# A lookup-and-MLP kernel: one token in 64 fetched row by row by SyncE, output stores on ScalarE, the last five tiles as blocks of one

## The chip, the cores and the metric

The kernel runs on one core of a Trainium2 chip. The metric is the device time of one execution in microseconds (us). Before the change it is 5179.57 us, the median of three runs (5178.03 to 5191.77). A core has five engines with a queue of instructions each, executed in order: TensorE (PE; its weight loads are shown as PEld), VectorE (DVE), ScalarE (ACT), GpSimd (POOL) and SyncE (SP), which computes nothing and issues DMAs. They meet through semaphores. Sixteen DMA engines move the data. A DMA issued by POOL has its descriptors written by software on POOL; one issued by SP or ACT goes through a hardware queue.

## The reference, cut to what matters

For each of 16384 samples, 32 token rows of 300 numbers are averaged, three groups of 20 small-table rows of 64 numbers are averaged, four more rows are looked up, and the 748 features go through three layers and a sigmoid. All of it is float32.

```
tok = word_emb[token_idx].mean(axis=1)          # 32 of 50000 rows of 300
e1 = emb_mh1[mh1_idx].mean(axis=1)              # 20 of 1000 rows of 64; e2, e3 likewise
emb = jnp.concatenate([tok, e1, e2, e3, o1, o2, o3, o4], axis=1)
wide = wide_mh1[mh1_idx].sum(axis=(1, 2)) + ...
h = jax.nn.relu(emb @ W1 + b1)                  # 748 -> 1024
h = jax.nn.relu(h @ W2 + b2)                    # -> 512
h = jax.nn.relu(h @ W3 + b3)                    # -> 256
return jax.nn.sigmoid(h @ Wd + bd + wide)
```

## The kernel before, in words

The samples are cut into 128 tiles of 128. Three streams of work are written out side by side, in one loop over `n_steps` = 128 x 11 + 27 = 1435 steps (L632); nothing reorders them afterwards, so what is written first on an engine runs first there.

**Small tables.** In the 11 steps of a tile the kernel counts how often each table row occurs in each sample. `one_hots` (L341) makes one-hot vectors on DVE for the next step (L348) and scales a part of them on ACT (L355); `counts` (L358) multiplies them on PE (L366), and ACT moves the counts from PSUM to SBUF (L369). In the tile after, `small_sums` (L381) multiplies counts with the tables on PE, 138 matmuls a tile in four groups, each into the one `pg` buffer (L401), and DVE takes each group from there (L391). The one-hots have `HOT_BUFS` = 3 buffers.

**Tokens.** `tokens` (L273) works in groups of two tokens, 16 a tile. For each token POOL issues one indirect DMA that gathers 128 rows of 1200 bytes, one per partition (L283). Three groups later (`TOK_LAG`) `add_up` (L260) adds both rows to a running sum on DVE (L264, L266, L271). `TOK_BUFS` = 6 groups have buffers. The loop hands these out at an even pace:

```
toks.to(n_all * (step + 1) / n_steps)          # n_all = 128 * 16 + 3 groups
```

**Layers.** When a tile's features are complete, PE transposes them and DVE scales them into the block's `x` (L442, L446). A block is three tiles (384 columns), but the last two tiles are blocks of one. `mlp` (L521) runs the layers of a block on PE (L505), ACT applies bias and relu (L516). Its matmuls are spread over the steps until `deadline` (L607), the step at which the next block is ready; the last block of three has until 6 steps before the end. `finish` (L542) adds the wide term on DVE (L544), takes the sigmoid on ACT (L545) and stores the outputs with a DMA on SP (L547).

**SP's queue** holds the loads of indices for each two tiles (`load_indices`, L294: one `it` for the tokens, L299; two `ix` for the tables, L304), tables and weights at the start, and the output stores. The semaphores of DMAs issued by SP and ACT are eight, taken in turn; a DMA waits for the one that had the semaphore before it.

Of the kernel before, what the change touches and what calls it, by code (L numbers as in the profile page):

```python
# [8 lines left out]
F32 = mybir.dt.float32  # L9
BF16 = mybir.dt.bfloat16  # L10
FP8 = mybir.dt.float8e3
I32 = mybir.dt.int32
# [6 lines left out]
P = 128  # L19
N_TOK, TOK_D = 32, 300  # L20
# [3 lines left out]
TOK_GROUP = 2  # L24
TOK_LAG = 3
TOK_BUFS = 6
HOT_BUFS = 3
WAKE = 27
EARLY = 3
LAST_LAYERS = 6  # L30
BLOCK = 256
LAYER_TILES = 3
LAST_TILES = 2
HALF = P // 2
UPPER = 256.0
COUNT = 64.0
# [4 lines left out]
STEPS = -(-HALF // ONEHOT)  # L41
# [22 lines left out]
def kernel(  # L64
# [21 lines left out]
    nc = tc.nc  # L86
    B = out.shape[0]
# [6 lines left out]
    for f in SMALL:  # L94
        n = -(-tables[f].shape[0] // P)
# [3 lines left out]
    tokp = ctx.enter_context(tc.tile_pool(name="tok", bufs=TOK_BUFS))  # L99
# [3 lines left out]
    scp = ctx.enter_context(tc.tile_pool(name="sc", bufs=2))  # L103
    ohp = ctx.enter_context(tc.tile_pool(name="onehot", bufs=HOT_BUFS))
    cp = ctx.enter_context(tc.tile_pool(name="counts", bufs=2))
    gp = ctx.enter_context(tc.tile_pool(name="g", bufs=3))
    wp = ctx.enter_context(tc.tile_pool(name="wide", bufs=2))
    xp = ctx.enter_context(tc.tile_pool(name="x", bufs=2))
# [19 lines left out]
    NK = len(chunk_rows)  # L128
# [126 lines left out]
    n_groups = N_TOK // TOK_GROUP  # L255
    n_all = B // P * n_groups + TOK_LAG
# [2 lines left out]

    def add_up(t, q, rows):  # L260

        a, b = rows[:, 0:TOK_D], rows[:, TOK_D : 2 * TOK_D]
        if q == 0:
            nc.vector.tensor_add(tok_sum, a, b)  # L264
        else:
            nc.vector.tensor_add(tok_sum, tok_sum, a)  # L266
            to = tok_sum
            if q == n_groups - 1:
                to = features(t)[:, TOK_AT:G_COLS]
                summed.add(t)  # L270
            nc.vector.tensor_add(to, tok_sum, b)  # L271

    def tokens():  # L273

        under_way = []
        for n in range(n_all):
            if n < n_all - TOK_LAG:
                t, q = divmod(n, n_groups)
                it = token_indices[t // NSUB][:, t % NSUB, :].bitcast(U32)
                rows = tokp.tile([P, TOK_GROUP * TOK_D], F32, name="tok_rows")  # L280
                for r in range(TOK_GROUP):
                    j = q * TOK_GROUP + r
                    nc.gpsimd.indirect_dma_start(  # L283
                        out=rows[:, r * TOK_D : (r + 1) * TOK_D],
                        out_offset=None,
                        in_=word,
                        in_offset=bass.IndirectOffsetOnAxis(ap=it[:, j : j + 1], axis=0),
                    )
                under_way.append((t, q, rows))
            if n >= TOK_LAG:  # L290
                add_up(*under_way.pop(0))
            yield 1

    def load_indices(blk):  # L294

# [110 lines left out]
    def wide_term(g):  # L406
# [7 lines left out]
        )  # L414
        nc.vector.tensor_add(g[:, WIDE_AT : WIDE_AT + 1], wide, g[:, 0:1])

    class Block:

        def __init__(self, first, n):
            self.first, self.n, self.missing = first, n * P, NK * n
            if first + n < B // P:
                self.x = xp.tile([P, NK, N], F32, name="x")
            else:
                self.x = cp.tile([P, NK, n * P], F32, name="x_last", tag="counts")

        def transpose(self, t, ks):

# [91 lines left out]
    def mlp(block, part=None):  # L521


        n = block.n
        flush_rows()
        h1 = hp.tile([P, M1, N], F32, name="h1", tag="odd")
        yield from layer(h1, w1_sb, b1_sb, [block.chunk(k) for k in range(NK)], M1, part)
        h2 = hp.tile([P, M2, N], F32, name="h2", tag="even")
        yield from layer(h2, w2_sb, b2_sb, [h1[:, k, 0:n] for k in range(M1)], M2)
        flush_outputs()  # L530
        h3 = hp.tile([P, M3 + 1, N], F32, name="h3", tag="odd")
        yield from layer(h3, w3_sb, b3_sb, [h2[:, k, 0:n] for k in range(M2)], M3)
        po = ps_h.tile([1, N], F32, name="po", tag="ph")
        for k in range(M3):
            if k == M3 - 1:
                flush_outputs()
            nc.tensor.matmul(  # L537
                po[:, 0:n], wd_sb[:, k : k + 1], h3[:, k, 0:n], start=(k == 0), stop=(k == M3 - 1)
            )
            yield 1  # L540

        def finish():  # L542
            y = h3[0:1, M3, 0:n]
            nc.vector.tensor_add(y, po[:, 0:n], block.wide())  # L544
            nc.scalar.activation(y, y, AF.Sigmoid, bias=bd_sb)  # L545
            b0 = block.first * P
            nc.sync.dma_start(out=out[b0 : b0 + n, :].rearrange("n o -> o n"), in_=y)  # L547

        rows_out.append(finish)

# [50 lines left out]
    block_of = {}  # L601

    def ready(t):

        return max(-(-(n_groups * (t + 1) + TOK_LAG) * n_steps // n_all) + 1, (t + 2) * STEPS + 2)

    def deadline(block):  # L607

        last = block.first + block.n // P
        ahead = tiles - 1 - last  # L610
        if ahead == 1 and block.n > P:
            return n_steps - LAST_LAYERS
        return ready(ends[last] - 1) if ahead > 0 else n_steps

    def block_for(t):
        if t not in block_of:
# [7 lines left out]
    toks = Paced(tokens())  # L624
# [6 lines left out]
    layers, cnt, sums, waiting, complete = None, None, None, [], []  # L631
    for step in range(n_steps):  # L632
        t, i = divmod(step, STEPS)
        s = t % NSUB
        blk = t // NSUB + 1
        more = blk * NSUB < tiles
# [34 lines left out]
        if complete and (layers is None or layers.done >= layers.total or complete[0].first + complete[0].n // P < tiles - 1):  # L671
# [6 lines left out]
            begin, left = step, max(deadline(block) - step, 1)  # L678
        toks.to(n_all * (step + 1) / n_steps)
        if t < tiles and more and s == 1 and i == 5:  # L680
            next_sc, evict = key_columns(next_keys)
            later.append((step, evict))
        ahead = 0
        if sums:
            ahead = n_h * (i + 1) / STEPS - sums_done[i + 1]
# [65 lines left out]
```

## Time and profile before

| | |
|---|---|
| median of three runs | 5179.57 us |
| the profiled execution | 5177.48 us |
| its span | 5175.7 us |
| PE busy | 4786.2 us, 92% |
| POOL busy | 3875.7 us, 75% |
| DVE busy | 3732.3 us, 72% |
| ACT busy | 2719.7 us, 53% |
| mean busy share of the 16 DMA engines in mid-run | 0.47 |
| share of the granted TensorE clock | 0.99 |

A line of the costliest groups gives the source line, the engine, the operation, what is written and read, the count, then busy time and mean ns, then the idle time of the engine just before these instructions and what ended most of it ("issue": nothing that the profile shows). A line of waits gives who waited for whom: us in total, times, the longest. A timeline line gives start, duration, engine, line, what is written and read, the count, and in brackets the idle time before it. SPq is SP's queue of DMA issues.

### The profile page before, as it was taken

The numbers are of one execution on the slowest core, as the hardware profiler recorded it, in microseconds if no ns is written. First come the engines' busy times: TensorE is split into PE (matmuls) and PEld (weight loads), VectorE is DVE, ScalarE is ACT, GpSimd is POOL, SyncE is SP. The second block draws the span as 40 slices with busy tenths as digits, with TensorE's granted clock in tenths as the row PEclk, the third lists the DMA queues.
The fourth block names the chain that finished last, engine by engine and source line by source line (L and its number), as shares of the span: only waits on it lengthen the run. The fifth ranks groups of instructions, "written<-read, shape, count | busy, mean of one in ns | idle before, by whom it ended". The sixth has DMA issues, their size and how long they took to land.

```text
span 5175.7 us, 92043 instructions
## 1 busy us (share of the span) xinstructions
PE 4786.2 (92%) x34812; PEld 3524.4 (68%) x34812; DVE 3732.3 (72%) x6656; ACT 2719.7 (53%) x3538; POOL 3875.7 (75%) x4103
## 2 busy tenths in 40 slices
PE   7799999999999999999999999999999999999999
PEld 4666666667667666767666766666667666667666
DVE  6777777777777777777777777777777777777773
ACT  6555555555555555555555555555555555555551
POOL 6777777777777777777777777777777777777775
PEclk9999999999999999999999999999999999999999
DMA  7444444444444444444444444444444444444443
GB/s 193 125 126 125 125 126 125 126 125 125 125 126 124 126 125 126 125 126 125 125 126 124 126 124 126 125 126 124 126 125 125 126 125 126 125 125 125 125 124 86
DMA packets 253982, 651.96 MB, mean 126 GB/s; under 512 B 120135, under 2 KB 120691, under 8 KB 253535
## 3 DMA queue, kind: packets, MB, share of 16 engines
q0 software_dynamic: 196608, 629.41, 45.4%
q1 hardware_dynamic: 56927, 16.66, 1.4%
q8 instruction: 272, 4.46, 0.4%
q14 instruction: 175, 1.43, 0.1%
HBM read 645.59 MB, written 0.07 MB: 125 GB/s over the span
## 4 chain that ended last, share of the span: by engine, by line
PE 49%; DMA 17%; DVE 15%; issue 11%; POOL 7%; ACT 0%; DVEq 0%; POOLq 0%; ACTq 0%
PE ph L505 27%; DMA tok_rows<-in_word_emb_dram,it 17%; PE pg L401 14%; POOL tok_rows L283 7%; DVE hot L348 5%; PE pc L366 5%; DVE own L271 4%; DVE own L266 3%; DVE g L391 2%; PE po L537 1%; PE pc L442 1%; DVE own L264 0%; DVE x L446 0%; ACT hot L355 0%; DVE ix L317 0%
## 5 line engine op out<-in xcount | busy, mean ns | idle before, releaser
L283 POOL DMA_INDIRECT tok_rows<-in_word_emb_dram,it x4096 | 3874.8, 946 | 1258.2 <-issue 788.3
L355 ACT ACTIVATE hot<-hot 64x768 bf16<-64x768 bf16 (+1 forms) x1408 | 1155.4, 821 | 1689.3 <-DVE hot L348 1676.8
L401 PE MATMUL pg<-terms,cnt 128*128 128x195 bf16 x17664 | 1734.8, 248 | 324.7 <-DVE g L391 324.7
L401 PEld LDWEIGHTS <-cnt 128*128 128x128 fp8e3 x17664 | 1519.2, 98 | 50.8 <-issue 32.4
L505 PE MATMUL ph<-x,w_sb 128*128 128x384 f32 (+2 forms) x4128 | 1476.8, 490 | 17.4 <-DVE x L446 17.1
L348 DVE TENSOR_TENSOR hot<-own,sc 128x1656 bf16<-128x1656 bf16 (+1 forms) x1408 | 1392.9, 989 | 83.3 <-PE pc L366 3.7
L369 ACT ACTIVATE cnt<-pc 128x828 uint16<-128x828 f32 (+1 forms) x1408 | 1185.8, 842 | 420.5 <-PE pc L366 398.8
L505 PE MATMUL ph<-h,w_sb 128*128 128x384 f32 (+1 forms) x3520 | 1238.7, 488 | 0.0
L271 DVE TENSOR_TENSOR own<-own,tok_rows 128x300 f32<-128x300 f32 x1792 | 856.9, 478 | 400.8 <-DMA tok_rows<-in_word_emb_dram,it 354.3
L505 PEld LDWEIGHTS ph<-x,w_sb 128*128 128x128 f32 (+1 forms) x4128 | 718.6, 191 | 556.0 <-issue 203.9
L266 DVE TENSOR_TENSOR own<-own,tok_rows 128x300 f32<-128x300 f32 x1920 | 917.7, 478 | 246.4 <-DMA tok_rows<-in_word_emb_dram,it 188.6
L366 PEld LDWEIGHTS <-hot 128*128 128x128 bf16 x8192 | 597.5, 97 | 511.9 <-issue 285.6
L505 PEld LDWEIGHTS ph<-h,w_sb 128*128 128x128 f32 x3520 | 619.5, 193 | 434.3 <-issue 150.8
L366 PE MATMUL pc<-hot 128*128 128x138 bf16 x8192 | 731.8, 225 | 28.6 <-ACT hot L355 23.4
L516 ACT ACTIVATE h<-ph,b_sb 128x384 f32<-128x384 f32 (+1 forms) x611 | 349.7, 572 | 280.0 <-PE ph L505 260.1
L391 DVE TENSOR_REDUCE g<-pg 128x130 f32<-128x390 f32 (+1 forms) x512 | 261.1, 510 | 324.1 <-PE pg L401 321.7
L446 DVE TENSOR_TENSOR x<-pc,scale 128x768 f32<-128x768 f32 x127 | 121.2, 954 | 107.3 <-PE pc L442 106.5
L264 DVE TENSOR_TENSOR own<-tok_rows 128x300 f32<-128x300 f32 x128 | 61.2, 478 | 87.7 <-DMA tok_rows<-in_word_emb_dram,it 86.3
L442 PE MATMUL pc<-ident,g 128*128 128x128 f32 x762 | 106.4, 277 | 0.4 <-ACT cnt L369 0.4
L335 DVE COPY sc<-pc 128x512 bf16<-128x512 bf16 x64 | 44.1, 689 | 80.5 <-PE pc L331 80.4
L442 PEld LDWEIGHTS pc<-ident,g 128*128 128x128 f32 x762 | 84.5, 143 | 16.3 <-issue 7.7
L271 DVE TENSOR_TENSOR g<-own,tok_rows 128x300 f32<-128x300 f32 x128 | 60.2, 470 | 34.8 <-DMA tok_rows<-in_word_emb_dram,it 32.1
(56 smaller groups left out, 404.9 us busy)
## 6 DMA issues: line engine op xcount, KB each, us to landing
tok_rows<-in_word_emb_dram,it POOLq DMA_INDIRECT x4096
ix<-in_idx_dram SPq DMA_DIRECT2D x128, 32.0 KB
w_sb<-in_W_dram SPq DMA_DIRECT2D x6, 512.0 KB
raw<-in_mh_dram SPq DMA_DIRECT2D x4, 682.5 KB
it<-in_idx_dram SPq DMA_DIRECT2D x64, 32.0 KB
w_sb<-in_W_dram SPq DMA_DIRECT2D x1, 2048.0 KB
out_dram<-h SPq DMA_DIRECT2D x42, 1.5 KB
raw<-in_mh_dram SPq DMA_DIRECT2D x2, 227.5 KB
```

The source lines that it names most:

```text
L266: nc.vector.tensor_add(tok_sum, tok_sum, a)
L271: nc.vector.tensor_add(to, tok_sum, b)
L283: nc.gpsimd.indirect_dma_start(out=rows[:, r * TOK_D : (r + 1) * TOK_D], out_offset=None, in_=word, in_offset=bass.IndirectOffsetOnAxis(ap ...
L348: nc.vector.tensor_tensor(hot[:, 0 : 2 * rows, :].rearrange("p i (n d) -> p i n d", d=2), iota.rearrange("p (n d) -> p n d", d=2).unsqueez ...
L355: nc.scalar.activation(upper, upper, AF.Copy, scale=UPPER)
L366: nc.tensor.matmul(pc[:, k // n, at : at + n_h], hot[:, 2 * k, 0:P], hot[:, 2 * k + 1, :], start=True, stop=True)
L369: nc.scalar.activation(cnt[:, :, b : b + rows].rearrange("l h (g k) -> l h g k", g=2), pc[:, :, 0 : n * n_h].rearrange("l g (k h) -> l h g ...
L391: nc.vector.tensor_reduce(field_columns(features(t), pair), pg[:, 0:n, :].rearrange("p f (c d) -> p f d c", c=3), AX.X, ALU.add,)
L401: nc.tensor.matmul(pg[:, j, :], by_slice[:, h, :], terms[:, h, :], start=(h == h0), stop=(h == h1 - 1))
L442: nc.tensor.transpose(pt[:, j // n, j % n, :], g[:, c : c + P], ident)
L505: nc.tensor.matmul(ph[:, 0:n], weights[: src.shape[0], k, m * P : (m + 1) * P], src, start=(k == 0), stop=(k == len(srcs) - 1),)
L516: nc.scalar.activation(dst[:, m, 0:n], ph[:, 0:n], AF.Relu, bias=bias[:, m : m + 1])
```

## The change

In tiles 4, 6, 8, ... 126, POOL gathers 31 tokens instead of 32. The rows of the last token are fetched by SP: `load_column` brings the 128 indices onto one partition, `fetch` reads them into SP's registers, 16 at a time, and issues one DMA per row, with an address computed from the register. This is written out over 20 steps, from 24 steps before the tile's sum is due; the column's load comes 4 steps earlier. `add_up` takes the two operands of a group from wherever they are.

Output stores are issued by ACT. The one-hots have two buffers in place of three. Tokens are handed out at two groups a step for the first 24 steps and at (2051 - 48) / (1435 - 24) = 1.4196 a step after that. The last five tiles are blocks of one; the last block of three gets 20 steps for its layers, each single block 8; the singles' `x` lie in pairs in a buffer of the counts. In tile 1 the columns of the next keys come four steps later.

```
-HOT_BUFS = 3
+HOT_BUFS = 2
+FETCH_FROM = 4
+FETCH_STEPS = 20
+FETCH_AHEAD = 24
+COLUMN_AHEAD = 4
+LOADS = 16
-LAST_LAYERS = 6
-LAST_TILES = 2
+LAST_TILES = 5
+FRONT_STEPS = 24
+FRONT_PACE = 2.0
+BLOCK_STEPS = 20
+TILE_STEPS = 8
...
+    fp = ctx.enter_context(tc.tile_pool(name="fetched", bufs=2))
...
-        a, b = rows[:, 0:TOK_D], rows[:, TOK_D : 2 * TOK_D]
+        a, b = rows
...
+                    if j == N_TOK - 1 and t in fetched:
+                        rows.append(fetched.pop(t))
+                        continue
+                    rows.append(tok_rows[:, r * TOK_D : (r + 1) * TOK_D])
...
+    def load_column(t):
+        columns[t] = fp.tile([1, P], I32, name="column")
+        nc.sync.dma_start(
+            out=columns[t], in_=idx[t * P : (t + 1) * P, N_TOK - 1 : N_TOK].rearrange("n o -> o n")
+        )
+
+    def fetch(t):
+        rows = fp.tile([P, TOK_D], F32, name="fetched")
+        column = columns.pop(t)
+        for p0 in range(0, P, LOADS):
+            _, values = nc.values_load_multi_w_load_instructions(
+                column[:, p0 : p0 + LOADS],
+                engines=[mybir.EngineType.SP],
...
+            for i, value in enumerate(values):
+                p = p0 + i
+                nc.sync.dma_start(out=rows[p : p + 1, :], in_=word[bass.ds(value, 1), :])
+                if p == P - 1:
+                    fetched[t] = rows
+                yield 1
...
-            if first + n < B // P:
+            if first + n + 2 < B // P:
                 self.x = xp.tile([P, NK, N], F32, name="x")
             else:
-                self.x = cp.tile([P, NK, n * P], F32, name="x_last", tag="counts")
+                if first + 2 == B // P or not last_x:
+                    last_x[:] = [cp.tile([P, 2, NK, P], F32, name="x_last", tag="counts")]
+                self.x = last_x[0][:, (first + 1) % 2]
...
-            nc.sync.dma_start(out=out[b0 : b0 + n, :].rearrange("n o -> o n"), in_=y)
+            nc.scalar.dma_start(out=out[b0 : b0 + n, :].rearrange("n o -> o n"), in_=y)
...
+    front = FRONT_STEPS * FRONT_PACE
+    pace = (n_all - front) / (n_steps - FRONT_STEPS)
+    fetches = [(int(summed_at(t)) - FETCH_AHEAD, t) for t in range(FETCH_FROM, tiles, 2)]
...
-        ahead = tiles - 1 - last
-        if ahead == 1 and block.n > P:
-            return n_steps - LAST_LAYERS
-        return ready(ends[last] - 1) if ahead > 0 else n_steps
+        if last < tiles - LAST_TILES:
+            return ready(ends[last] - 1)
+        return begin + (BLOCK_STEPS if block.n > P else TILE_STEPS)
...
-        toks.to(n_all * (step + 1) / n_steps)
+        for at, t_f in fetches:
+            if step == at - COLUMN_AHEAD:
+                load_column(t_f)
+            if step == at:
+                fetching.append((at, Paced(fetch(t_f))))
+        for at, rows in list(fetching):
+            rows.to(P * (step + 1 - at) / FETCH_STEPS)
...
+        toks.to(tokens_by(step + 1))
-        if t < tiles and more and s == 1 and i == 5:
+        if t < tiles and more and s == 1 and i == (5 if t > 1 else 9):
```

More of the change, by code (lines that the diff above doesn't have):

```diff
@@ L279, in tokens @@
                 it = token_indices[t // NSUB][:, t % NSUB, :].bitcast(U32)
-                rows = tokp.tile([P, TOK_GROUP * TOK_D], F32, name="tok_rows")
+                tok_rows = tokp.tile([P, TOK_GROUP * TOK_D], F32, name="tok_rows")
+                rows = []
                 for r in range(TOK_GROUP):
                     j = q * TOK_GROUP + r
+                    if j == N_TOK - 1 and t in fetched:
+                        rows.append(fetched.pop(t))
+                        continue
+                    rows.append(tok_rows[:, r * TOK_D : (r + 1) * TOK_D])
                     nc.gpsimd.indirect_dma_start(
-                        out=rows[:, r * TOK_D : (r + 1) * TOK_D],
+                        out=rows[-1],
                         out_offset=None,
@@ L292, in tokens @@
             yield 1
+    fetched, columns = {}, {}
+    def load_column(t):
[10 more added lines that the diff above has]
+                engines=[mybir.EngineType.SP],
+                min_val=0,
+                max_val=word.shape[0] - 1,
+                skip_runtime_bounds_check_because="the indices are rows of the table",
+            )
+            for i, value in enumerate(values):
[4 more added lines that the diff above has]
+                yield 1
     def load_indices(blk):
@@ L415, in wide_term @@
         nc.vector.tensor_add(g[:, WIDE_AT : WIDE_AT + 1], wide, g[:, 0:1])
+    last_x = []
     class Block:
@@ L601, with tokens_by, summed_at, deadline @@
     block_of = {}
+    front = FRONT_STEPS * FRONT_PACE
+    pace = (n_all - front) / (n_steps - FRONT_STEPS)
+    def tokens_by(step):
+        return min(FRONT_PACE * step, front + pace * (step - FRONT_STEPS))
+    def summed_at(t):
+        n = n_groups * (t + 1) + TOK_LAG
+        return n / FRONT_PACE if n < front else FRONT_STEPS + (n - front) / pace
     def ready(t):
-        return max(-(-(n_groups * (t + 1) + TOK_LAG) * n_steps // n_all) + 1, (t + 2) * STEPS + 2)
-    def deadline(block):
+        return max(-int(-summed_at(t) // 1) + 1, (t + 2) * STEPS + 2)
+    fetches = [(int(summed_at(t)) - FETCH_AHEAD, t) for t in range(FETCH_FROM, tiles, 2)]
+    fetching = []
+    def deadline(block, begin):
         last = block.first + block.n // P
-        ahead = tiles - 1 - last
-        if ahead == 1 and block.n > P:
-            return n_steps - LAST_LAYERS
-        return ready(ends[last] - 1) if ahead > 0 else n_steps
+        if last < tiles - LAST_TILES:
+            return ready(ends[last] - 1)
+        return begin + (BLOCK_STEPS if block.n > P else TILE_STEPS)
     def block_for(t):
@@ L670 @@
                     complete.append(block)
-        if complete and (layers is None or layers.done >= layers.total or complete[0].first + complete[0].n // P < tiles - 1):
+        if complete and (layers is None or layers.done >= layers.total or complete[0].first < tiles - LAST_TILES):
             flush(step)
@@ L677 @@
             layers.total = mlp_work * layers.size
-            begin, left = step, max(deadline(block) - step, 1)
-        toks.to(n_all * (step + 1) / n_steps)
-        if t < tiles and more and s == 1 and i == 5:
+            begin, left = step, max(deadline(block, step) - step, 1)
+        for at, t_f in fetches:
[5 more added lines that the diff above has]
+            rows.to(P * (step + 1 - at) / FETCH_STEPS)
+            if step + 1 - at >= FETCH_STEPS:
+                rows.finish()
+                fetching.remove((at, rows))
+        toks.to(tokens_by(step + 1))
+        if t < tiles and more and s == 1 and i == (5 if t > 1 else 9):
             next_sc, evict = key_columns(next_keys)
```

## The prediction

> **What bounds the kernel now.** I read the page's busy line first: TensorE (PE) looks like the bound at 92%.
>
> ```profile
> span 5175.7 us, 92043 instructions
> PE 4786.2 (92%) x34812; PEld 3524.4 (68%) x34812; DVE 3732.3 (72%) x6656; ACT 2719.7 (53%) x3538; POOL 3875.7 (75%) x4103
> L283 POOL DMA_INDIRECT tok_rows<-in_word_emb_dram,it x4096 | 3874.8, 946 | 1258.2 <-issue 788.3
> ```
>
> The third line, from the costliest groups, corrects this. POOL's 4096 token gathers are 3874.8 us busy, and the idle time before them is 1258.2 us: together 5133 of 5176 us. That idle time is no waiting: it is 0.31 us before each gather. The view of busy time by stage shows whether it is ever anything else.
>
> ```profile
> 40.00:80.00 40.00, 36.94 (x227) 22.84 (x226) 15.08 (x25) 31.05 (x51) 24.79 (x27) 1.00 0.79 214
> 1000.00:2000.00 1000.00, 935.11 (x6880) 690.17 (x6878) 733.34 (x1303) 533.46 (x687) 756.45 (x800) 1.00 0.47 125
> 3000.00:4000.00 1000.00, 934.62 (x6810) 688.53 (x6808) 733.97 (x1303) 531.01 (x685) 756.57 (x800) 0.99 0.47 125
> ```
>
> Columns are PE, weight loads, DVE, ACT, POOL. 800 gathers in 1000 us, stage after stage: one per 1.25 us without exception. POOL is the bound. Only at the start does it miss a beat: 27 gathers instead of 32 in 40 to 80 us, and 30 in 80 to 120 us (same view), so 7 x 1.25 = 8.75 us. The labels "DVE" on many of POOL's waits mean nothing: they too last 0.3 us.
>
> Next I read the view of waits, for who is second.
>
> ```profile
> DVE own L271 <- DMA tok_rows<-in_word_emb_dram,it: 354.3, 567, 2.9
> PE pg L401 <- DVE g L391: 324.7, 257, 4.7
> DVE own L266 <- DMA tok_rows<-in_word_emb_dram,it: 188.6, 265, 2.6
> ```
>
> With the first and last add of a tile (86.3 and 32.1 us), DVE stands 661 us waiting for gathered rows: DVE has room. PE has little: of 1000 us it is busy 934, and nearly all the rest is one wait, for DVE to empty the only pg buffer. The timeline shows that part of this can't go away:
>
> ```profile
> 2514.26 1.80 PE L401 MATMUL pg<-terms,cnt 128*128 128x195 bf16 x19
> 2516.10 0.56 DVE L391 TENSOR_REDUCE g<-pg 128x130 f32<-128x390 f32 x1 [1.96 <-PE pg L401]
> 2516.72 0.24 PE L401 MATMUL pg<-terms,cnt 128*128 128x195 bf16 x1 [0.65 <-DVE g L391]
> ```
>
> DVE was idle and took the sum at once, and PE still stood 0.65 us, because the next matmul needs the same buffer. That is the least such a wait costs; it comes twice a tile (257 waits in 128 tiles).
>
> **The change, part by part.** The sum is made against the profiled execution: 5177.48 us, its span 5175.7 plus 1.8, and 2.1 below the median of 5179.57.
>
> *One gather less in tiles 4, 6, ... 126.* 62 gathers leave POOL: 62 x 1.25 = -77.5 us. The adds on DVE stay as they are.
>
> *The same rows through SP.* For each of these tiles SP loads a column of 128 indices, reads them into registers by 16, and issues 128 copies of one 1200-byte row each. No such copy is in the trace. The nearest rows are SP's own issues, in the views of single lines (durations in ns, least/median/most):
>
> ```profile
> L547 SPq DMA_DIRECT2D out_dram<-h x44: 227/267/280, 296.8 to 5173.4; - x44
> L304 SPq DMA_DIRECT2D ix<-in_idx_dram x128: 533/592/1767, 1.3 to 4838.8; - x128
> L304 SPq EVENT_SEMAPHORE  x106: 17/28/1349, 11.3 to 4826.1; - x106
> ```
>
> What time is there? Two tiles hold 63 gathers of POOL, 78.75 us. SP also loads the indices of two tiles (0.38 + 2 x 0.59 us, waits and the column: about 2.5 us). So a row may cost (78.75 - 2.5) / 128 = 0.596 us before SP is later than POOL. From below a row is one plain issue, 0.27 us, plus a gap of 0.05 us between issues (SP's timeline at the start): 0.32. From above it is an issue like that of ix, 0.59, with three register instructions at 0.07 each (one wait instruction of 28 ns and its gap) and an index read that takes a whole index load, 2.1 us issue to landing, shared by 16: 0.59 + 0.05 + 0.21 + 0.13 = 0.98 us. I take the nearest: the output store is also one piece of one partition (1536 bytes), so 0.27 + 0.05, two register instructions 0.14, and 0.06 for the read: 0.52 us, 69 us in two tiles. Then SP ends nothing, and this costs 0; the margin is 15%, which is thin. Each copy on a semaphore also waits for the copy eight before it; an output store lands 1.4 to 1.7 us after its issue, an index load 2.1 to 2.8 us, so eight in flight allow one per 0.35 us at worst. The copies' data are 128 x 1200 bytes beside 63 gathers of the same size, on queues that are 47% busy: hidden.
>
> The Trainium skill speaks against this part: "DMA: Bandwidth & Descriptors", section "Rules for kernel authors", says to coalesce many small transfers into one large one. By the store's row the price is SP's time and SP is idle, so I set the rule aside; by the rule alone the sum would lose its largest term. The same page gives about 0.6 us as the least time of a register load ("Latency and other measured facts"); no run here shows it. My estimate from it: one load per 16 indices is 0.04 us a row, and SP keeps up; one load per index is 0.6 us, and SP is the bound.
>
> *Who waits for SP.* The last group's second add takes the fetched row, and behind it on DVE stand the next one-hot and the sum evictions. The fetch is written out in 20 steps, ending 4 steps (14 us) before that add, so a lag of SP under 14 us is hidden.
>
> *Output stores move from SP to ScalarE.* 46 issues of 0.27 us plus the wait for the sigmoid just before (0.4 to 0.6 us): under 40 us on an engine that is idle 47%; what stands behind are hot and cnt, two steps early. 0; at most 0.5 us x 46 = 23 if every one hit PE. On SP they had to go: its view of waits has 3637.9 us for them, and rows would have stood behind them.
>
> *HOT_BUFS 3 to 2.* In 13% of the steps of this trace a one-hot starts before the counts two steps back have ended, by 0.7 us on average; those starts now wait. The one-hot is used some 4 us later, so I take 0; if all of it reached PE it would be 121 us less what DVE's 661 us absorb.
>
> *The front: two groups a step for 24 steps.* The adds come earlier in DVE's order, buffers stand empty when DVE waits long for PE. Gain 0 to 8.75 us; I take -8.
>
> *Can the others follow?* A step (one turn of the loop) needs 2051 / 1435 = 1.429 groups of two gathers now, 3.574 us. After the front it is (2051 - 48) / (1435 - 24) = 1.4196, times 63/64: 3.494 us, 2.2% less. PE is busy 0.9335 x 3.574 = 3.336 us of a step; two least waits a tile are 2 x 0.65 / 11 = 0.118. Together 3.454: PE follows with 0.04 to spare. With the waits as they are (324.7 / 1435 = 0.226) it is 3.562, and 1411 steps x 0.068 = 96 us eat the gain whole. Which? Part of the excess over 0.65 is DVE standing for rows that now come earlier, part is DVE busy with one-hot and adds. I take +20 us; ends 0 and +96.
>
> *The last five tiles alone.* A matmul pass on 384 columns takes 0.326 us (14.69 / 45), on 128 columns 0.112 (8.3 / 72, timeline of the end): three singles 59.1 us against 57.4, so 1.7 us. What counts is the order:
>
> ```profile
> 5133.60 0.95 POOL L283 DMA_INDIRECT tok_rows<-in_word_emb_dram,it  x1 [0.30 <-issue]
> 5137.95 0.47 DVE L271 TENSOR_TENSOR g<-own,tok_rows 128x300 f32<-128x300 f32 x1 [2.13 <-DMA tok_rows<-in_word_emb_dram,it]
> 5152.12 0.55 PE L442 MATMUL pt<-ident,g 128*128 128x128 f32 x3
> 5172.93 0.40 ACT L545 ACTIVATE h<-h,bd_sb 1x128 f32<-1x128 f32 x1 [0.78 <-DVE h L544]
> ```
>
> The last tile's sum is there at 5138.4, but PE turns to it at 5152.1: 13.7 us behind other tiles' layers. With these done earlier the tail shrinks by 0 to 13.7; I take -10. The price lies before it: the last block of three now has 20 steps, the next single 8, while counts still run. 28 steps x (3.454 - 57.4 / 33) = 48 us, plus 57.4 and 19.7, is 125 us of PE in 98 us of POOL. 27 us late, of which six row buffers hide some 10 to 15: +12, ends 0 and +17.
>
> **Sum:** -77.5 - 8 + 20 - 10 + 12 = -63.5. Span 5112, time 5114 us; 1.2% faster.
>
> **Rivals.** (1) SP becomes the bound: slower. Its place is the row copy, and it decides from 0.61 us a row: the first fetch starts near 100 us, the last ends some 65 us before the end, and 62 x (128 x 0.61 + 2.5) + 165 = 5161 us, and past the present 5176 from 0.612. At 0.66 us (ix's issue and one register instruction) it is 62 x 87 + 165 = 5560. For it: 15% margin on a price no row shows. Against: the store's 0.27. Chance 0.21. (2) PE becomes the bound and eats the gain: -77.5 - 8 + 96 - 10 + 12 = +12.5, so 5175 to 5190. For it: 93% busy. Against: DVE's 661 us of standing for rows. Chance 0.07. (3) The fetch does what it says, but SP trails by more than 14 us here and there, and ScalarE's stores, which take the same eight semaphores, wait for SP's copies with hot and cnt behind them: 2 us at each of 46 stores would be 92 us on 5114, so 5115 to 5206. Chance 0.06, half of it slower than before.
>
> **How the numbers follow.** Forecast 0.66, its own range 5078 (all terms at their good end: -77.5 - 8.75 - 13.7) to 5155 (PE's term +60). With rival 3's half and some of rival 2, faster by over 0.3% is 0.69. Within 0.3%, about what a measurement of this kernel can tell from no change: 0.07. Slower: 0.24, nearly all SP. To leave out no more than 2 in 10, the range goes up to 5300, SP at 0.627 us a row.
>
> **What would show it.** POOL: 4034 gathers, still 1.25 us apart; 32 in 40 us from the start on. SP: 7936 row copies, pitch near 0.52 us and idle between fetches; if they follow each other without a gap through the whole span, rival 1. DVE's waits for rows fall from 661 us, and none is long on "fetched". PE above 94% with the wait for g near 0.65 to 1 us; if instead POOL's gathers have gaps in mid-run and PE is at 96%, rival 2. From the last gather to the end some 30 us in place of 41. Wrong I am if the register reads and address arithmetic on SP cost more than the store's row suggests.

## The result, and the profile after

The changed kernel takes 5155.68 us (median of six runs, 5152.52 to 5158.6); the kernel before, in the same comparison, 5179.22 us. The ratio is 0.9954, 95% interval 0.9943 to 0.9965: 0.46% faster, where 1.2% was forecast. The profiled execution took 5156.35 us, its span 5154.6 us, 21.1 us less than before.

The page's first lines and the group of the gathers:

```profile
span 5154.6 us, 117390 instructions
PE 4797.3 (93%) x35172; PEld 3556.2 (69%) x35172; DVE 3752.9 (73%) x6658; ACT 2733.7 (53%) x3568; POOL 3819.6 (74%) x4041
L297 POOL DMA_INDIRECT tok_rows<-in_word_emb_dram,it x4034 | 3818.7, 947 | 1307.0 <-issue 887.1 <-DVE own L280 141.3 <-DVE own L275 92.6
```

62 gathers are gone, and one takes 947 ns (946 before), but the idle time in front of them has grown from 1258.2 to 1307.0 us. Busy time by stage (columns as in the prediction) shows where:

```profile
40.00:80.00 40.00, 33.73 (x174) 18.91 (x173) 22.94 (x40) 28.85 (x48) 30.25 (x33) 0.91 0.74 186
1000.00:2000.00 1000.00, 941.50 (x6873) 692.60 (x6873) 739.39 (x1306) 537.35 (x690) 744.18 (x787) 0.99 0.46 125
2000.00:3000.00 1000.00, 947.96 (x6907) 697.15 (x6906) 741.98 (x1310) 539.56 (x692) 743.60 (x786) 0.99 0.46 125
3000.00:4000.00 1000.00, 944.56 (x6943) 696.93 (x6942) 750.67 (x1327) 542.69 (x700) 755.46 (x799) 0.99 0.47 127
4950.00:5000.00 50.00, 48.69 (x308) 34.37 (x307) 28.11 (x47) 21.83 (x29) 29.20 (x31) 1.00 0.34 94
5000.00:5050.00 50.00, 46.23 (x431) 41.62 (x430) 28.48 (x54) 24.47 (x41) 29.64 (x33) 1.00 0.36 99
```

The start no longer misses a beat: 33 gathers stand in its window. From 1000 to 3000 us there are 787 and 786 gathers per 1000 us instead of 800, and near 5000 us only 31 and 33 in 50 us instead of 40. From 3000 to 4000 us all is as forecast: 799, with TensorE at 94.5%.

Adding up, from the starts of all gathers in the traces, what each distance is longer than the usual 1.251 us gives a ledger. (Only distances longer by over 0.2 us count as stops. "End stops" are those in the last 230 us of gathering.)

| us | before | after | difference | forecast |
|---|---|---|---|---|
| gathers x 1.25 | 4096 | 4034 | -77.5 | -77.5 |
| stops before 300 us | 9.5 | 0.0 | -9.5 | -8 |
| stops in mid-run | 1.3 | 54.4 | +53.1 | 0 for SP, +20 for TensorE |
| end stops | 0.0 | 24.0 | +24.0 | +12 |
| last gather's start to the end | 42.1 | 28.3 | -13.8 | -10 |
| sum | | | -23.7 | -63.5 |

The span fell by 21.1; the other 2.6 us are gathers that stand 0.0006 us further apart. The sum misses the forecast by 42 us: the stops in mid-run are 33 us over their row and those at the end 12 us, while the front and the tail are 1.5 and 4 us better than forecast. The waits name the first:

```profile
DVE g L280 <- DMA fetched<-in_word_emb_dram: 104.7, 19, 12.9
DVE own L280 <- DMA tok_rows<-in_word_emb_dram,it: 63.5, 96, 2.3
PE pg L444 <- DVE g L434: 243.9, 256, 8.0
DVE hot L391 <- PE pc L409: 213.0, 258, 3.8
```

VectorE waits 104.7 us for rows that SP fetched, at 19 of 62 tiles. Six buffers of gathered rows hide about half of that from GpSimd. SP's own view of waits says what SP was doing meanwhile:

```profile
SPq L332 <- DMA out_dram<-h: 819.8, 42, 53.6
```

A row copy stands for an output store of ScalarE, 42 times, 19.5 us on average. The timeline of tile 48 shows one such stand and all that follows from it:

```profile
1943.46 1.04 SPq L332 DMA_DIRECT2D fetched<-in_word_emb_dram  x3
...
1967.00 0.61 ACT L592 ACTIVATE h<-h,bd_sb 1x384 f32<-1x384 f32 x1 [1.95 <-DVE h L591]
1967.64 0.21 ACTq L594 DMA_DIRECT2D out_dram<-h  x1
...
1969.30 2.67 SPq L332 DMA_DIRECT2D fetched<-in_word_emb_dram  x7
...
1977.78 0.94 POOL L297 DMA_INDIRECT tok_rows<-in_word_emb_dram,it  x1 [0.30 <-issue]
...
1982.95 0.47 DVE L280 TENSOR_TENSOR g<-own,fetched 128x300 f32<-128x300 f32 x1 [11.34 <-DMA fetched<-in_word_emb_dram]
...
1985.13 0.95 POOL L297 DMA_INDIRECT tok_rows<-in_word_emb_dram,it  x1 [6.41 <-DVE own L273]
```

SP issues no row from 1944.3 to 1969.3 us. It goes on 1.7 us after ScalarE's store. The last 25 rows take it to 1981.5; VectorE had wanted them since 1971.6; GpSimd runs out of free row buffers and stands for 6.1 us beyond its usual 0.31. The stand began after row 102 of the fetch (counted from 0). In the code the next row, which stands, belongs to step 536, and the store to step 543 (counted by the one-hots that ScalarE scales in front of it, one a step). So a row copy waits for a store that the code issues some seven steps, 24 us, later. The eight semaphores were not dealt in the order of the steps: in the built program the store has its turn between rows 95 and 96 of this fetch, so row 103, eight turns on, takes its semaphore. The operands in the trace bear this out: row 95 names semaphore 101, the store 102 and row 96 103, and row 103 names 102 again. So it goes through the whole trace: at 41 of the 46 stores SP has stood for 6 to 54 us, and it goes on 1.1 to 1.9 us after the store is issued, each time with a row copy that names the store's semaphore.

SP's price per row is not the trouble. Its lines, durations in ns (least/median/most):

```profile
L332 SPq FUSED_REGOPS  x7936: 37/37/51, 108.8 to 5093.0; - x199
L332 SPq MOVE fetched<-in_word_emb_dram x7936: 29/29/39, 108.9 to 5093.1; - x199
L332 SPq DMA_DIRECT2D fetched<-in_word_emb_dram x7936: 224/225/313, 108.9 to 5093.1; - x199
L323 SPq TENSOR_LOAD <-column x496: 1132/1231/1482, 107.3 to 5085.6; - x166
```

A fetch without a stand takes 65.4 us (tile 44, 1740.0 to 1805.4), 0.515 us a row. 0.52 was forecast.

The end of the kernel, the lines that answer to those of before:

```profile
5126.28 0.95 POOL L297 DMA_INDIRECT tok_rows<-in_word_emb_dram,it  x1 [0.30 <-issue]
5129.18 0.47 DVE L280 TENSOR_TENSOR g<-own,tok_rows 128x300 f32<-128x300 f32 x1 [0.63 <-DMA tok_rows<-in_word_emb_dram,it]
5131.00 0.55 PE L489 MATMUL pt<-ident,g 128*128 128x128 f32 x3
5151.80 0.40 ACT L592 ACTIVATE h<-h,bd_sb 1x128 f32<-1x128 f32 x1 [0.78 <-DVE h L591]
```

TensorE now turns to the last tile 1.4 us after its sum is done, where before it came 13.7 us late.

### The profile page after: what moved, and what is told of

It reads as the page before. It is cut to its first block, busy times and chain, and to the rows that moved or that the text cites. A ratio compares the mean times of both kernels' runs of the same rounds, so it can differ in the third digit from the quotient of the medians.

```text
span 5154.6 us, 117390 instructions
## 1 busy us (share of the span) xinstructions
PE 4797.3 (93%) x35172; PEld 3556.2 (69%) x35172; DVE 3752.9 (73%) x6658; ACT 2733.7 (53%) x3568; POOL 3819.6 (74%) x4041
## 4 chain that ended last, share of the span: by engine, by line
PE 79%; DVE 8%; issue 4%; DMA 4%; SPq 3%; POOL 1%; ACT 0%; DVEq 0%; POOLq 0%; ACTq 0%
PE ph L552 42%; PE pg L444 26%; PE pc L409 8%; DMA tok_rows<-in_word_emb_dram,it 3%; DVE g L434 2%; SPq L332 2%; DVE hot L391 2%; PE pc L489 1%; DVE own L280 1%; DVE own L275 1%; POOL tok_rows L297 1%; PE po L584 1%; SPq L323 1%; DMA fetched<-in_word_emb_dram 0%; DVE x L493 0%
## 5 line engine op out<-in xcount | busy, mean ns | idle before, releaser
L297 POOL DMA_INDIRECT tok_rows<-in_word_emb_dram,it x4034 | 3818.7, 947 | 1307.0 <-issue 887.1
L444 PE MATMUL pg<-terms,cnt 128*128 128x195 bf16 x17664 | 1742.1, 249 | 243.9 <-DVE g L434 243.9
L552 PE MATMUL ph<-h,w_sb 128*128 128x384 f32 (+1 forms) x3680 | 1223.1, 469 | 0.0
L280 DVE TENSOR_TENSOR own<-own,tok_rows 128x300 f32<-128x300 f32 x1792 | 856.8, 478 | 123.0 <-DMA tok_rows<-in_word_emb_dram,it 63.5
L378 DVE COPY sc<-pc 128x512 bf16<-128x512 bf16 x64 | 44.2, 691 | 131.1 <-PE pc L374 130.7
L280 DVE TENSOR_TENSOR g<-own,fetched 128x300 f32<-128x300 f32 x62 | 29.2, 470 | 108.9 <-DMA fetched<-in_word_emb_dram 104.7
```

Source lines behind the costliest of these rows:

```text
L297: nc.gpsimd.indirect_dma_start(out=rows[-1], out_offset=None, in_=word, in_offset=bass.IndirectOffsetOnAxis(ap=it[:, j : j + 1], axis=0),)
L444: nc.tensor.matmul(pg[:, j, :], by_slice[:, h, :], terms[:, h, :], start=(h == h0), stop=(h == h1 - 1))
L552: nc.tensor.matmul(ph[:, 0:n], weights[: src.shape[0], k, m * P : (m + 1) * P], src, start=(k == 0), stop=(k == len(srcs) - 1),)
```

## The experiments

On some of the chips that the runs fell on, the kernel before took 7413 to 7473 us, at a granted clock near 0.86 in place of 0.99. The runs there stand together at the end. Every run is compared with the kernel before on its own chip.

**Without the row copies.**

```
-FETCH_FROM = 4
+FETCH_FROM = 128
```

> Changed kernel without the row copies: all 4096 gathers are issued again, and front, tail, two hot buffers and stores on ScalarE stay. Theory A (the gathers at 1.25 us set the time wherever nothing is late): +77.5 us for 62 gathers, -53 us of mid-run stops, so 5170 to 5182 us on a chip where the kernel before takes 5180. Rival B (TensorE at two hot buffers sets the stops): the stops stay, 5200 to 5235 us. Where TensorE is the bound (the kernel before at 7400 us) it is faster than the kernel before by 4%, as in the two calls before.

5176.55 us against 5178.36; ratio 0.9998, 0.9988 to 1.0008. Mid-run stops 1.5 us, end stops 20.9 us, 28.2 us behind the last gather. Two of its stages:

```profile
1000.00:2000.00 1000.00, 941.40 (x6849) 690.24 (x6849) 739.63 (x1311) 536.95 (x693) 756.60 (x800) 1.00 0.46 125
4950.00:5000.00 50.00, 48.69 (x307) 34.39 (x306) 28.04 (x48) 21.85 (x29) 31.81 (x34) 1.00 0.38 105
```

So the mid-run stops belong to the fetch, as theory A has it. Two hot buffers cost nothing in mid-run, and the end stops are there without the fetch. The rest of the change nets about 2 us: 9.5 gained at the start, 14 behind the last gather, 21 lost in end stops.

**The fetch begun 12 steps earlier.**

```
-FETCH_AHEAD = 24
+FETCH_AHEAD = 36
```

> Changed kernel with the row copies begun 36 steps ahead of their use instead of 24 (126 us instead of 84). Theory A (SP's copies come late because SP stands for ScalarE's output stores, up to 54 us a fetch; the late rows stop the gathers for 53 us in mid-run): the fetch now has 126 - 65 = 61 us of slack, which covers even the longest stand; VectorE's wait for the fetched rows falls from 104.7 us to under 10 and GpSimd's stops in mid-run from 53 us to under 10, so the run falls from 5156 to 5100 to 5115 us. Rival B (TensorE or VectorE, not the rows, sets those stops): the wait for the rows goes but the stops stay with another cause beside them, 5145 to 5160 us. Where TensorE is the bound (as in the two calls before, where the kernel before took 7413 and 7473 us), both say no change.

5237.27 us against 5178.36; ratio 1.0112, 1.0095 to 1.0129. This is a miss of both theories: 82 us slower than with 24. Waits, of SP and of VectorE, and a group of VectorE:

```profile
SPq L332 <- DMA out_dram<-h: 881.9, 41, 37.5
...
DVE low L359 <- DMA ix<-in_idx_dram: 127.8, 20, 11.6
```

```profile
L280 DVE TENSOR_TENSOR g<-own,fetched 128x300 f32<-128x300 f32 x62 | 29.1, 470 | 2.7 <-DVE own L275 0.5 <-DMA fetched<-in_word_emb_dram 0.2
```

The rows are no longer late: 0.2 us of waiting in place of 104.7. But SP stands for the stores as long as ever, and so its copies come forward by only half of what was asked: on average a fetch starts 86 gathers before its add, with 24 steps it was 68, which is 23 us earlier instead of 42. The index loads for the small tables are written at the same steps as before, and now up to 12 steps' worth of rows that SP can't issue so early stand in front of them: they are issued 14 gathers, 18 us, later on average. VectorE waits 127.8 us for these indices, where it waited 2.0, and GpSimd's mid-run stops rise to 130 us. Starting earlier moved the lateness from the rows to the indices; the stands had to go.

**Only the last block's outputs stored.**

```
-            nc.scalar.dma_start(out=out[b0 : b0 + n, :].rearrange("n o -> o n"), in_=y)
+            if b0 + n == B:
+                nc.scalar.dma_start(out=out[b0 : b0 + n, :].rearrange("n o -> o n"), in_=y)
```

> Changed kernel in which only the last block's outputs are stored (45 of 46 stores left out, so the output is not the reference's). Theory A2 (after the run with the fetch begun 36 steps ahead, which moved the row copies hardly at all: SyncE is never free there, it stands 20 us at two of three fetches for ScalarE's store of a block, since a row copy must wait for the store whose turn of the eight shared DMA semaphores it takes; the stands, not the place of the fetch in the code, make the rows late): no stands, the rows are in 15 us and more before use, VectorE's wait for the fetched rows falls from 104.7 us to under 10, GpSimd's stops in mid-run from 53 us to under 10, and the time to 5095 to 5115 us. Rival B2 (SyncE is late by its own work or by what its index loads wait for): the stands go, the wait for the rows stays over 60 us, 5140 to 5160 us.

5112.42 us against 5191.46; ratio 0.9848, 0.9832 to 0.9864. Mid-run stops 1.7 us. SP's longest total of waits, and VectorE's wait for the rows:

```profile
SPq L347 <- DVE keys L364: 676.7, 58, 17.0
```

```profile
L280 DVE TENSOR_TENSOR g<-own,fetched 128x300 f32<-128x300 f32 x62 | 29.2, 470 | 2.8 <-DMA fetched<-in_word_emb_dram 0.4 <-DVE own L275 0.3
```

SP now runs so far ahead that it stands, harmlessly, for the buffer of the next index load. It has time to spare: theory A2.

**All outputs stored, from SP, 12 steps after they are ready.**

```
+            late = block.first < B // P - LAST_TILES
+            y = block.wide() if late else h3[0:1, M3, 0:n]
...
+                stores.append((now[0] + STORE_AFTER, to, y))   # STORE_AFTER = 12
...
+        if stores and step >= stores[0][0]:
+            _, to, y = stores.pop(0)
+            nc.sync.dma_start(out=to, in_=y)
```

> Changed kernel with all outputs stored, but those of the blocks of three tiles from SyncE's own queue, 12 steps (42 us) after ScalarE has them; they are kept in the block's row of x until then. On one queue there is no store of another queue to stand for, and the output is long done when the store's turn comes. Theory A2: SyncE stands for no store, late rows under 10 us, 5095 to 5115 us, as with the stores left out. Rival B2: 5140 to 5160 us.

5113.83 us against 5191.46; ratio 0.9851, 0.9835 to 0.9868. Mid-run stops are 2.3 us. The time is as theory A2 has it, one of its reasons is not. SP still stands for ScalarE:

```profile
SPq L706 <- ACT x L595: 609.1, 40, 24.4
```

```profile
L281 DVE TENSOR_TENSOR g<-own,fetched 128x300 f32<-128x300 f32 x62 | 29.1, 470 | 2.1
```

609 us of standing, and no row is late: VectorE is idle for 2.1 us in all before these 62 adds. Standing as such costs nothing, then; what counts is whether SP has time enough behind it.

**One word undone: stores from SP, at once.**

```
-            nc.scalar.dma_start(out=out[b0 : b0 + n, :].rearrange("n o -> o n"), in_=y)
+            nc.sync.dma_start(out=out[b0 : b0 + n, :].rearrange("n o -> o n"), in_=y)
```

> The changed kernel with the stores on SyncE's queue again, on a chip where TensorE is not the bound, if this is one (the kernel before at 5180 to 5192 us). Theory A2 (the place among the row copies at which SyncE stands makes rows late): late rows under 15 us, mid-run stops under 12, ratio 0.985 to 0.988. Rival E (stands on ScalarE as such make rows late): late rows over 60 us, ratio 0.993 to 0.997.

5105.4 us against 5180.04; ratio 0.9855, 0.9838 to 0.9871: 50 us better than the changed kernel, for one word. Mid-run stops are 2.0 us. SP's waits, and two stages:

```profile
SPq L594 <- ACT h L592: 833.2, 46, 45.1
```

```profile
1000.00:2000.00 1000.00, 954.71 (x6994) 702.38 (x6993) 752.00 (x1329) 547.66 (x704) 756.29 (x799) 1.00 0.47 128
3000.00:4000.00 1000.00, 947.62 (x6967) 699.74 (x6965) 752.55 (x1331) 543.28 (x700) 756.35 (x800) 0.99 0.47 128
```

SP stands 833 us for ScalarE, longer than the 819.8 us of the changed kernel, and rival E falls: no row is late (0.3 us of waiting for the fetched rows in all). On its own queue the store has its place where the code put it. When SP reaches it ahead of ScalarE, SP is ahead of everything, and the rows behind the store are those of later steps. The fetch for tile 48 runs from 1849.1 to 1914.1 us without a stop and is used at 1939.9.

**The end of the kernel: two more steps for the last block of three.** On the kernel with late stores:

```
-BLOCK_STEPS = 20
+BLOCK_STEPS = 22
```

> The kernel with late stores, and the last block of three tiles spread over 22 steps instead of 20. Theory C (the 21 to 24 us of GpSimd's stops near 5000 us, which the kernel without row copies has too, are TensorE's: 20 steps of 3.3 us with all but 20 of 33 parts of a block's layers in them, about 70 us of TensorE, come to 66 + 28 = 94 us where the gathers want 70): two more steps take about 5 us off these stops, so 4 to 6 us less than the kernel with late stores alone. Rival (the stops come from a buffer that the single tiles want): no change.

5112.5 us against 5191.46; ratio 0.9847, 0.983 to 0.9863, not to be told from late stores alone. End stops 20.2 us against 23.3: 3 us, less than theory C's 5. This run settled nothing.

**The last block of three with 40 matmul passes less.** On late stores; this kernel leaves out five of the six chunks of that block's first layer, so the results of its three tiles are not the reference's:

```
-        ... [block.chunk(k) for k in range(NK)], M1, part)
+        ... [block.chunk(k) for k in range(1 if block.short else NK)], M1, part)
```

> The kernel with late stores, in which the last block of three leaves out five of the six chunks of its first layer (40 passes of 384 columns, some 15 to 20 us of TensorE; the outputs of these three tiles are wrong for it). Theory C: TensorE has that much less to do in the 20 steps, GpSimd's stops near 5000 us fall from 24 to 5 to 10 us, and the time by 14 to 19 us against late stores alone (ratio 0.981 to 0.983). Rival D (a wait that is not TensorE's work sets the stops): no change, 0.985.

5091.22 us against 5191.53; ratio 0.9807, 0.9791 to 0.9823. The end stops are gone altogether, 0.0 us where theory C had 5 to 10, and the time is 22.6 us less where it had 14 to 19: the 40 passes are 80 MATMULs in the profile, and TensorE's busy time fell by 25 us (4781.4 to 4756.4), more than the expected 15 to 20. The same 100 us with late stores alone, then with the short layer:

```profile
4900.00:4950.00 50.00, 48.69 (x307) 34.41 (x306) 28.61 (x49) 21.95 (x29) 28.72 (x32) 1.00 0.35 96
4950.00:5000.00 50.00, 47.89 (x456) 43.72 (x455) 28.36 (x52) 24.47 (x41) 31.19 (x34) 1.00 0.37 103
```

```profile
4900.00:4950.00 50.00, 48.05 (x419) 40.23 (x418) 36.08 (x62) 27.39 (x40) 37.82 (x41) 1.00 0.46 127
4950.00:5000.00 50.00, 47.31 (x467) 45.90 (x466) 25.08 (x52) 14.08 (x29) 37.81 (x41) 1.00 0.45 125
```

TensorE is busy 48.69 of 50 us in the first, GpSimd makes 32 and 34 gathers. With 25 us of TensorE's work taken away GpSimd makes 41 and 41. The end stops are TensorE's work, which rival D denied.

**Two last tiles as blocks of one, as before.** On late stores:

```
-LAST_TILES = 5
+LAST_TILES = 2
+LAST_LAYERS = 6
...
-        if last < tiles - LAST_TILES:
-            return ready(ends[last] - 1)
-        return begin + (BLOCK_STEPS if block.n > P else TILE_STEPS)
+        ahead = tiles - 1 - last
+        if ahead == 1 and block.n > P:
+            return n_steps - LAST_LAYERS
+        return ready(ends[last] - 1) if ahead > 0 else n_steps
```

> The kernel with late stores, with the end of the kernel before: two last tiles as blocks of one instead of five, and its due times for them. Theory C (three more tiles whose layers run as passes of 128 columns, which TensorE can take no faster than their weight loads of 0.191 us, 33 us a tile against 21 us a tile in a block of three, and 94 us of TensorE in the last block's 20 steps, make the 21 to 24 us of GpSimd's stops near 5000 us): these stops fall to under 4 us, GpSimd's last gather comes 20 us earlier, what follows it grows from 28 to 42 us, so 4 to 10 us less than with late stores alone: 0.9835 of the kernel before, against 0.9851 there. Rival D (the stops come from the front's order or the two hot buffers, and five last tiles are worth their 14 us): stops stay, ratio 0.987 to 0.989.

This kernel left out the store of the last block of three, whose turn came behind the loop. 5110.27 us against 5191.53; ratio 0.9843, 0.9829 to 0.9856. End stops 2.3 us in place of 23.3, 43.6 us behind the last gather in place of 28.4: by the ledger 6 us better than late stores alone, in the time some 4. Theory C's price of a single tile, 33 us by weight loads of 0.191 us, is not borne out: weight loads overlap, and in the trace of the kernel before 80 passes of 128 columns in a row take 9.15 us (L505, from 5162.59 us), 0.114 us each and so 20 us for a tile's 176. TensorE's busy time hardly depends on the number of single tiles either: 4781.4 us with five and 4781.9 with two, where theory C has 36 us between them. That leaves the order of the work, above all the 20 steps for the last block of three; the number of single tiles and their due times were not changed apart.

**Both undone: stores from SP, two last tiles.** What is left of the change is the fetch, the front and two hot buffers.

> The changed kernel with two of its parts undone: stores on SyncE's queue, and the end of the kernel before (two last tiles as blocks of one). Left of the change are the row copies, the new front and two hot buffers. From the ledger: against the kernel with SyncE's stores alone (5105 us, 0.9855) the end stops fall from 25 to 2 us and the time behind the last gather grows from 28 to 42 us, so 5 to 9 us less: 5096 to 5101 us where a gather is 1.251 us, ratio 0.984. Rival D (five last tiles are worth their 14 us): 0.987 or more.

5096.8 us (5096.02 to 5098.79) against 5178.21; ratio 0.9843, 0.983 to 0.9856. This is the fastest complete kernel of the study, 1.6% under the kernel before and some 59 us under the changed one. Its page and its last stages:

```profile
span 5097.0 us, 116630 instructions
PE 4777.5 (94%) x34812; PEld 3518.1 (69%) x34812; DVE 3751.1 (74%) x6656; ACT 2726.5 (53%) x3538; POOL 3820.3 (75%) x4041
```

```profile
4915.00:4965.00 50.00, 45.81 (x307) 32.68 (x306) 35.95 (x66) 25.31 (x33) 37.81 (x41) 0.97 0.47 127
4965.00:5015.00 50.00, 48.69 (x255) 32.12 (x254) 22.10 (x50) 5.84 (x10) 37.80 (x41) 1.00 0.46 125
```

Stops of 2.6 us in mid-run and 2.3 at the end, 44.2 us behind the last gather. GpSimd's 4034 gathers at 1.251 us are now all of its time but that tail.

**The runs beside a kernel before of 7413 to 7473 us.** Four on the first such chip, with edits told above:

> The changed kernel with FETCH_AHEAD 24 -> 36: every row copy is written out 12 steps earlier, so it stands ahead of the output store that it now waits behind. Theory (rows come late because SP's copies share eight semaphores with the stores and stand until ScalarE has issued the store): DVE's wait for fetched falls from 104.7 us to under 10, POOL's stops in mid-run (53 us in the changed kernel) vanish, span 5100 to 5115. Rival 1 (SP is simply too slow at 0.49 us a row): the waits shift but stay above 60 us, span 5145 to 5155. Rival 2 (PE at 94% is the bound anyway): the wait for fetched vanishes, but the span stays above 5140 and the wait of PE for g grows by what POOL gains.

> The changed kernel without its output stores, but for the last block's (outputs of the other blocks are left out). Takes away the one thing SP stands for, and nothing else of note (46 issues of 0.27 us on ScalarE). Theory: SP's longest wait falls from 53.6 us to under 5, SP runs ahead up to its two buffers, wait for fetched under 10 us, span 5095 to 5115. Rival 1 (SP too slow): each fetch still takes its 65 us and lateness stays above 60 us in total, span 5145 or more. Rival 2 (PE): lateness gone, span above 5140.

> The changed kernel with the stores issued by SP again. Theory: the move to ScalarE did not free SP, since the eighth copy after a store waits for it in either case; SP now stands eight copies (4 us) earlier: wait for fetched 105 to 180 us, span 5150 to 5175. Rival (the move to ScalarE is what makes the fetch workable): SP stands far longer, wait for fetched over 400 us, span over 5250.

> The changed kernel with all 4096 gathers on POOL again (no tile is fetched); front, two one-hot buffers, ScalarE stores and the single last tiles stay. Theory: POOL works 77.5 us more and stops some 53 us less in mid-run: span 5170 to 5182, so the fetch is worth only about 20 us as it stands. Rival (two one-hot buffers and the closer wait for PE cost the time, not the late rows): span above 5195, with DVE's wait of hot for PE above 200 us as in the changed kernel.

Against 7473.48 us: 7486.79 with 36 steps (ratio 1.0021, 0.9998 to 1.0045), 7432.18 with few stores (0.9944, 0.993 to 0.9958), 7440.43 with SP's stores (0.9956, 0.9934 to 0.9978), 7173.86 without the fetch (0.9579, 0.9534 to 0.9623). Three on another:

> The changed kernel with FETCH_AHEAD 24 -> 36, on a chip that runs the kernel before near 5180 us (the first time it went to one on which PE's instructions came late and the kernel before took 7473 us). Theory (rows come late because SP's copies share eight semaphores with the stores and stand until ScalarE has issued the store): DVE's wait for fetched falls from 104.7 us to under 10, POOL's stops in mid-run (53 us) vanish, span 5100 to 5115. Rival 1 (SP is simply too slow at 0.49 us a row): waits stay above 60 us, span 5145 to 5155. Rival 2 (PE at 94% is the bound anyway): the wait vanishes, but the span stays above 5140.

> The changed kernel without its output stores, but for the last block's (the outputs of the other blocks are left out), on a chip of the first kind. Theory: SP's longest wait in mid-run falls from 53.6 us to under 5, wait for fetched under 10 us, span 5095 to 5115. Rival 1 (SP too slow): lateness above 60 us in total, span 5145 or more. Rival 2 (PE): lateness gone, span above 5140.

> The changed kernel with all 4096 gathers on POOL again, on a chip of the first kind. Theory: POOL works 77.5 us more and stops some 53 us less in mid-run: span 5170 to 5182, so the fetch is worth only about 20 us as it stands. Rival (two one-hot buffers and the closer wait for PE cost the time, not the late rows): span above 5195, with DVE's wait of hot for PE above 200 us as in the changed kernel.

Against 7412.79 us: 7407.49 (1.0003, 0.9984 to 1.0023), 7358.52 (0.9933, 0.9911 to 0.9954), 7094.73 (0.9569, 0.9531 to 0.9607). And two on a third, the first of them the kernel with two last tiles and late stores, with its missing store issued behind the loop:

```
+    for _, to, y in stores:
+        nc.sync.dma_start(out=to, in_=y)
     while complete or layers:
```

> Two last tiles as in the run before it, with the store of the last block of three, which that kernel left out, issued behind the loop: late stores, the fetch, the new front, and the end of the kernel before. Theory C: end stops 2 us, 43 us behind the last gather, 3 to 6 us less than late stores with five last tiles (ratio 0.984). Rival D: no better than with five, 0.985 or more.

> Changed kernel with the one word undone: outputs stored from SyncE's queue, with no delay. On one queue a store stands where the code issues it, some 7 to 9 steps (25 to 30 us) later among the row copies than the copy that stands for it in the changed kernel. Theory A2 (it is the place among the row copies at which SyncE must stand that makes rows late): SyncE still stands, but level with the code, rows are there 10 us and more before use, late rows under 15 us, mid-run stops under 12, 5100 to 5116 us where a gather is 1.251 us (ratio 0.985 to 0.988). Rival E (stands on ScalarE as such make rows late, wherever they are): late rows over 60 us, 5140 to 5165 us, ratio 0.993 to 0.997.

Against 7423.41 us: 7350.38 (0.99, 0.9882 to 0.9918) and 7375.96 (0.993, 0.991 to 0.9951). A stage of the run with few stores on the second chip, and two of its waits:

```profile
1000.00:2000.00 1000.00, 776.87 (x4812) 535.81 (x4810) 516.96 (x915) 375.69 (x482) 520.79 (x552) 0.88 0.32 88
```

```profile
POOL tok_rows L297 <- DVE own L280: 2056.0, 593, 14.8
...
PEld L444 <- issue: 662.2, 821, 6.9
```

552 gathers in 1000 us: GpSimd stands for VectorE, and TensorE is at a clock of 0.88 with long idle times that end in nothing the profile shows. The times expected of theory A don't apply where the gathers don't set the time. The changed kernel itself did not run here. Against the kernel before, the kernels without the stands or with harmless ones gain 0.4 to 1.0%, and the one that starts the fetch earlier gains nothing. Leaving the fetch out gains 4%, which the ledger does not explain. Why TensorE took longer in these runs, and why the fetch weighs so much there, was not found. It need not be the chip: the second of these chips carries number 5, and so does the one on which the kernel before took 5178.21 us beside the kernel with both parts undone; whether the two are the same is not known.

## Why the prediction was right and wrong

- *62 gathers less, -77.5:* right. The gathers kept their 1.25 us.
- *A row copy at 0.52 us, SP's 69 us in two tiles:* right, 0.515 us. One plain issue, two register instructions and a share of an index read was the right build-up. The index read is 1.23 us for 16, 0.077 us a row. The Trainium skill, page "DMA: Bandwidth & Descriptors", section "Latency and other measured facts", gives about 0.6 us as the floor of such a load; the load of 16 indices here took twice that, which a floor allows, so the floor was no price. The rule against many small transfers was rightly set aside: 7936 copies cost nothing where no row is late (mid-run stops of 2.0 us with the stores on SP).
- *"Output stores move from SP to ScalarE: 0. On SP they had to go":* **this is the step that failed.** It priced the move on the engine the stores went to, and there it did cost nothing (1.5 us of mid-run stops without the fetch, with ScalarE's stores). It read SP's 3637.9 us of waiting as a cost, though it was SP's spare time: back on its own queue SP stands 833 us and no row is late. It forgot SP's side of the shared semaphores, which the prediction had listed itself: a copy waits for the DMA that had its semaphore eight turns earlier, and that was now another engine's. In place of 0 the runs show 52 us: 54.4 us of mid-run stops with the stores on ScalarE, 2.0 with them on SP. Rival 3 had this coupling the wrong way round, with stores waiting for SP's copies. Undoing the move alone gave 50 us back.
- *"A lag of SP under 14 us is hidden":* true as a bound, but the lag was taken to come from SP's pace. It comes from stands of 19.5 us on average, 42 in 62 fetches, and VectorE still waited up to 12.9 us.
- *The end, +12 for the squeeze and -10 behind it:* TensorE's work in the last steps, as forecast, but both sizes too small: +24 and -14. The estimate let six row buffers hide 10 to 15 us of the 27 us it had found; 24 stood. So this part of the change loses 4 to 9 us net (the two comparisons with two last tiles) where it was put at a loss of 2.
- *The front, -8:* measured -9.5.
- *TensorE follows, +20:* too careful. With no row late, mid-run stops are 2 us at TensorE's 95%. The wait for the pg buffer fell from 324.7 to 243.9 us, 0.95 us each, and to 229.9 with the stores on SP.
- *HOT_BUFS, 0:* right. One-hots wait 213 us for TensorE, where they had waited 3.7, and the kernel without the fetch loses nothing in mid-run.
- *Rival 1,* SP as the bound by its price, didn't come: 65 us of work in two tiles, in 78.75.

With that one word left as it was the total comes near the forecast, 5105 us for 5114, but partly by luck: the +20 for TensorE did not come, and the end stops were 25 us in place of 12.

## What to carry to other kernels

When a DMA moves to another engine's queue, ask for every queue that shares its completion semaphores which of its DMAs comes next on the same semaphore: that one will wait for the moved DMA, even if the code issues it steps earlier. A long wait in an in-order queue is not a cost until something behind it is late; look for the first late consumer rather than for the largest wait. And if a transfer is late, find what its queue stands for before starting it earlier: here the earlier start brought the rows in time and made the index loads behind them late.

## What was not expected of the hardware

Gathers have two paces. Some executions have a gather every 1.251 us (mean 947 ns busy), some every 1.254 us (949 ns); the second lengthens the 4034 gathers by 12 us. Both came on one chip, one after the other (few stores at 1.254 us, late stores at 1.251): late stores took 5103.71 us in the profiled execution, at 1.251 us, and 5113 to 5116 us in the other three. The kernel before took 5177.27 us once there and 5191 to 5193 us otherwise, which would fit 4096 gathers, but there is no trace of these executions to show it. What sets the pace was not found. The 5113.83 us of late stores and the 5105.4 us of stores from SP at once are therefore no difference of the two edits: at one pace their spans are 5102.0 and 5104.6 us.
